# A Macaron block with its convolution by eight products for six outputs instead of six products for four

## The chip, the cores and the metric

The kernel runs on one core of a Trainium2 chip. The metric is the device time of one execution in microseconds. Time before: median 1013.6 us of three runs (1012.51 to 1014.02).

## The reference, cut to what matters

The input is one sequence of 2048 tokens of 1024 channels in fp32. The block adds half of a feed-forward layer, then a convolution with a block-wise causal attention, then half of the same feed-forward layer again:

```python
x = x + 0.5 * ffn(layernorm(x))
x = x + attention(layernorm(x))
x = x + 0.5 * ffn(layernorm(x))

def ffn(x):
    routing = softmax(x @ gate_w.T)                       # 8 experts
    return x * (routing @ in_channel_scale) @ sign(weight).T * (routing @ out_channel_scale) + bias

def attention(x):
    x = conv1d(x, conv_w, padding="SAME") + conv_b        # conv_w: (3, 1024, 768)
    q, k, v = split(x, 3, axis=-1)                        # 256 columns each
    qh, kh, vh = (project(t) for t in (q, k, v))          # 16 heads of 64
    p = softmax(causal(qh @ kh.T / 8))                    # inside blocks of 128 tokens
    return (p @ vh) @ wo + bo, projected by proj_w, plus proj_b
```

What the change touches most is the convolution of three taps from 1024 to 768 columns, between the first feed-forward layer and the attention.

## The kernel before

The program has four stages, one after the other: the first feed-forward layer (FFN1), the convolution, the attention, the second feed-forward layer (FFN2). It is written for a tile framework that follows data between the engines and orders each engine's instructions by program order and readiness; `pin(...)` keeps an instruction at its place in the program order. SyncE (SP) issues the plain transfers in its own queue order, and GpSimd (POOL) issues those that accumulate into their destination.

**FFN1** goes through 16 tiles of 128 tokens (`Ffn.run`). For each tile it normalises, transposes, routes, scales, and multiplies with the signs of the weights, `sw`, which are formed once at the start from eight loads and kept through the program. The products `pm_f` (line 286) are added to the residual row (lines 295 and 296). Behind each tile, `norm_x2` normalises the new row for the attention branch (`x2n`; its statistics in `normalize`, lines 157 to 170), and `transpose_x2` transposes it (`tr2`, line 398) into a window `xw` that holds the tile's tokens sorted by their place among four neighbours, plus one token at either end. The window is stored to DRAM (`win`), since it is needed again later.

**The convolution** is a Winograd form: from windows of inputs, six linear combinations V0 to V5 are formed on VectorE; from the three taps g0, g1, g2 of the weights, six combinations u0 to u5; the six products u_k times V_k are made on TensorE, and VectorE combines them into four neighbouring outputs. V0 and V5 (the "ends") need only g0 and g2 as weights, and their products are the groups `ce`; the others are `cv`. The 2048 tokens are processed in two halves of 1024 tokens, so a product has 256 columns. For each half, `conv_ends` makes the twelve end products (six blocks `w` of 128 output columns, two ends) while VectorE forms V1 to V4 from the reloaded windows (`load_pair`, `xl`); `conv_middle` then goes through the six blocks w with four products each, the taps of the next block (`taps`, lines 465 to 471), and the ten output operations (lines 540 to 549). All products share line 475:

```python
def product(half, acc, uk, k):
    for c in range(DC):                       # 8 chunks of 128 channels
        nc.tensor.matmul(acc..., lhsT=uk[:, c, :], rhs=V[half, k][:, :, c, :], ...)
```

V0 of the first half is formed while FFN1 runs, tile by tile (`end_transform`), and so is V5 of the first half (`store_window`).

**The attention** has four groups of 512 tokens and eight pairs of heads each, through five stages: `stage_qkv` (value products `pv`, line 716, into `vh`; query and key products `pq`, line 732), `stage_softmax`, `stage_transpose` (copies `pT`), `stage_values` (`ao`), `stage_wo`. The convolution's outputs come back from DRAM by `load_qkv`; group 0 lies in the first half. Residual rows `xr` are loaded in the second pair of each group into a ring of eight buffers (`rring`), and the result leaves as `x3`. The columns of `w` are 0 and 1 for queries, 2 and 3 for keys, 4 and 5 for values.

**FFN2** runs as FFN1 on the rows `x3`, with the same signs `sw`.

Of the kernel before, what the change touches and what calls it, by code (L numbers as in the profile page):

```python
# [24 lines left out]
def kernel(  # L25
# [52 lines left out]
    sw = fw.tile([P, DC, D], F32R, name="sw")  # L78
# [9 lines left out]
    up = pool(b1, "up", 1)  # L88
    vp0 = pool(b1, "vp0", 1)
    ends = b1.enter_context(ExitStack())  # L90
    vp5 = pool(ends, "vp5", 1, side="right")
    ring = b1.enter_context(ExitStack())
    xring = pool(ring, "xring", 8, side="right")
    xwp = pool(ring, "xwp", 3, side="right")
# [77 lines left out]
    class Ffn:  # L172
# [6 lines left out]
        def __init__(self, name, work, xnp, first, end, row, ahead, after, between, beside):  # L179
            self.name, self.work, self.xnp, self.first, self.end = name, work, xnp, first, end  # L180
            self.row, self.ahead, self.after, self.between, self.beside = row, ahead, after, between, beside
            self.xns, self.xnTs, self.lgps, self.routs, self.rTs, self.oscs, self.ys = ({} for _ in range(7))
# [95 lines left out]
        def main(self, t, *halves, between=None, at=DC - 2):  # L278
            y, osc, xrow = self.ys[t], self.oscs[t], self.row(t)
            pms = {h: bank("mm", [P, NB], f"pm_{self.name}_{t}_{h}") for h in halves}  # L280
            for c in range(DC):
                if between and c == at:
                    between()
                for h, pm in pms.items():
                    for n in range(2):
                        nc.tensor.matmul(  # L286
                            pm,
                            lhsT=y[:, n, c, :],
                            rhs=sw[:, c, ts(h, NB)],
                            start=(c == 0 and n == 0),  # L290
                            stop=(c == DC - 1 and n == 1),
                        )
# [57 lines left out]
    NK = 6  # L350
    SCALES = (1.0 / 4, -1.0 / 6, -1.0 / 6, 1.0 / 24, 1.0 / 24, 1.0)
    HALVES = 2
    TH = T // HALVES
    NQ = TH // 4
    QT = P // 4
    TPH = NT // HALVES

# [8 lines left out]
    LEFT, RIGHT = 3 * ROW - 1, QT  # L366
    AT = (LEFT, 0, ROW, 2 * ROW, LEFT + 1, 1)
    win_dram = [spill.tile([P, 2, DC, 4 * ROW], F32, name=f"win_{n}") for n in range(NT // 2)]
    x2, x2ns, xws, xls = {}, {}, {}, {}
    V = {(0, 5): vp5.tile([P, TPH, DC, QT], F32, name="v_0_5", tag="v5")}  # L370
    V |= {(half, 0): vp0.tile([P, TPH, DC, QT], F32, name=f"v_{half}_0") for half in range(HALVES)}

# [4 lines left out]
    def window(t):  # L377
        if t not in xws:
            xws[t] = xwp.tile([P, DC, 4 * ROW], F32, name=f"xw_{t}", tag="xw")
            nc.gpsimd.memset(xws[t][:, :, 2 * ROW - 1 :: 2 * ROW], 0.0)  # L380
            if t == 0:
                nc.gpsimd.memset(xws[t][:, :, LEFT : LEFT + 1], 0.0)
            if t == NT - 1:
                nc.gpsimd.memset(xws[t][:, :, RIGHT : RIGHT + 1], 0.0)
        return xws[t]
# [7 lines left out]
    def transpose_x2(t):  # L393
        xn, xw = x2ns.pop(t), window(t)
        for h in range(DC // 4):
# [3 lines left out]
            rows4 = xw[:, 4 * h : 4 * h + 4, :].rearrange("p c (k q) -> p c k q", q=ROW)  # L399
            nc.scalar.copy(rows4[:, :, :, 0:QT], tr.rearrange("p c (q k) -> p c k q", k=4))  # L400
        if t > 0:
            nc.gpsimd.tensor_copy(xws[t - 1][:, :, RIGHT : RIGHT + 1], xw[:, :, 0:1])
            store_window(t - 1)
        if t + 1 < NT:
            nc.gpsimd.tensor_copy(window(t + 1)[:, :, LEFT : LEFT + 1], xw[:, :, LEFT + QT : LEFT + ROW])
        end_transform(V[t // TPH, 0][:, t % TPH, :, :], xw, 0)
        if t + 1 == NT:
            store_window(t)

    def end_transform(v, xw, first):  # L410
        d0, d2, d4 = (xw[..., ds(at, QT)] for at in AT[first::2])
        nc.vector.scalar_tensor_tensor(v, d2, -5.0, d4, ALU.mult, ALU.add)
        nc.vector.scalar_tensor_tensor(v, d0, 4.0, v, ALU.mult, ALU.add)

    def store_window(t):
        xw = xws.pop(t)
        if t < TPH:
            end_transform(V[0, 5][:, t, :, :], xw, 1)
        nc.sync.dma_start(out=win_dram[t // 2][:, t % 2], in_=xw)

    def load_pair(n, tf):
        xls[n] = tf.tile([P, 2, DC, 4 * ROW], F32, name=f"xl_{n}", tag="xl", bufs=TPH // 2)
        nc.sync.dma_start(out=xls[n], in_=win_dram[n])

    def transform(n, k, tf):

        half, at = divmod(2 * n, TPH)
        _, d1, d2, d3, d4, _ = (xls[n][:, :, :, ds(at, QT)] for at in AT)
        v = [V[half, i][:, at : at + 2, :, :] if (half, i) in V else None for i in range(NK)]
        tmp = tf.tile([P, 2, DC, QT], F32, name=f"vt_{n}_{k}", tag="vt")  # L430
        if k == 1:
            nc.vector.scalar_tensor_tensor(v[1], d2, -4.0, d4, ALU.mult, ALU.add)
            nc.vector.scalar_tensor_tensor(tmp, d1, -4.0, d3, ALU.mult, ALU.add)
            nc.vector.tensor_tensor(v[2], v[1], tmp, ALU.subtract)
            nc.vector.tensor_tensor(v[1], v[1], tmp, ALU.add)
        else:
            nc.vector.tensor_tensor(v[3], d4, d2, ALU.subtract)
            nc.vector.tensor_tensor(tmp, d3, d1, ALU.subtract)
            nc.vector.scalar_tensor_tensor(v[4], tmp, -2.0, v[3], ALU.mult, ALU.add)
            nc.vector.scalar_tensor_tensor(v[3], tmp, 2.0, v[3], ALU.mult, ALU.add)  # L440

    def beside(t):

        if t >= NT - 3:
            for w in (2 * (t - NT + 3), 2 * (t - NT + 3) + 1):
                load_g(0, w, 0, pinned=True)
# [3 lines left out]
    def load_g(half, w, *taps, pinned=False):  # L450
        for j in taps:
            gs[half, w, j] = cwp.tile([P, DC, P], F32, name=f"g_{half}_{w}_{j}", tag="cw")
            ins = nc.sync.dma_start(out=gs[half, w, j], in_=conv_w[w, :, j])
# [3 lines left out]
    qkv_dram = [[spill.tile([P, TH], F32, name=f"qkv_{half}_{w}") for w in range(NW)] for half in range(HALVES)]  # L457

    def taps(half, w, ks):

        g = [gs[half, w, j] for j in range(3)]
        a, b = (up.tile([P, DC, P], F32, name=f"u_{half}_{w}_{k}", tag=f"u{k}") for k in ks)
        us.setdefault((half, w), {}).update(zip(ks, (a, b)))
        if ks[0] == 1:
            pin(nc.vector.tensor_tensor(a, g[0], g[2], ALU.add))
            nc.vector.tensor_tensor(b, a, g[1], ALU.subtract)
            nc.vector.tensor_tensor(a, a, g[1], ALU.add)  # L467
        else:
            nc.vector.scalar_tensor_tensor(a, g[2], 4.0, g[0], ALU.mult, ALU.add)
            nc.vector.scalar_tensor_tensor(b, g[1], -2.0, a, ALU.mult, ALU.add)  # L470
            nc.vector.scalar_tensor_tensor(a, g[1], 2.0, a, ALU.mult, ALU.add)

    def product(half, acc, uk, k):
        for c in range(DC):
            nc.tensor.matmul(  # L475
                acc.rearrange("p (t q) -> p t q", q=QT),
                lhsT=uk[:, c, :],
                rhs=V[half, k][:, :, c, :],
                start=(c == 0),
                stop=(c == DC - 1),  # L480
            )

    def leave(half, w, k, acc, mp):
        m = ms.setdefault((half, w), {})
        m[k] = mp.tile([P, NQ], F32, name=f"m_{half}_{w}_{k}", tag=f"m{k}", bufs=NW if k in (0, 5) else 1)
# [5 lines left out]
    def conv_ends(half, mp, tf, vp14):  # L491


        for k in range(1, 5):
            V[half, k] = vp14.tile([P, TPH, DC, QT], F32, name=f"v_{half}_{k}", tag=f"v{k}")
        pairs = range(half * TPH // 2, (half + 1) * TPH // 2)
        jobs = [lambda n=n: transform(n, 1, tf) for n in pairs]
        jobs += [lambda n=n: transform(n, 3, tf) for n in pairs]
        jobs += [lambda ks=ks: taps(half, 0, ks) for ks in ((1, 2), (3, 4))]
        if half > 0:  # L500
            V[half, 5] = vp5.tile([P, TPH, DC, QT], F32, name=f"v_{half}_5", tag="v5")
            ends = [V[half, 5][:, at : at + 2, :, :] for at in range(0, TPH, 2)]
            jobs = [lambda n=n, v=v: end_transform(v, xls[n], 1) for n, v in zip(pairs, ends)] + jobs
        for at in range(2 * NW):
            last, w = divmod(at, NW)
            if w % 2 == 0:
                acc = bank("mm" if at % 4 == 0 else "acc", [P, 2, NQ], f"ce_{half}_{last}_{w}")
            product(half, acc[:, w % 2, :], gs.pop((half, w, 2 * last)), 5 * last)
            leave(half, w, 5 * last, acc[:, w % 2, :], mp)
            if not last:  # L510
                load_g(half, w, 2)
            else:
                load_g(half, w // 3, w % 3)
# [421 lines left out]
```

## Time and profile before

One execution was profiled. It took 1014.76 us as a whole; the span between its first and last instruction was 1013.0 us, at a mean granted clock of 0.999.

| stage (us from the span's start) | length | TensorE busy | VectorE busy | ScalarE busy | GpSimd busy |
|---|---|---|---|---|---|
| FFN1, 0 to 200.1 | 200.1 | 185.66 | 153.43 | 113.98 | 92.64 |
| join, 200.1 to 206.9 | 6.8 | 6.06 | 3.00 | 2.75 | 1.20 |
| convolution, 206.9 to 453.9 | 247.0 | 245.76 | 174.75 | 25.75 | 0.46 |
| attention, 453.9 to 847 | 393.1 | 391.60 | 224.99 | 177.20 | 84.59 |
| FFN2, 847 to 1013 | 166.0 | 155.23 | 109.47 | 68.76 | 60.51 |

In the profile, PE is TensorE's matmuls, PEld its weight loads, DVE VectorE, ACT ScalarE, POOL GpSimd and SP SyncE. A group of instructions is given by its line, its engine, its operation, the names of what it writes and reads, the shape and the count; then follow its busy time, the mean duration of one in nanoseconds, and the idle time of its engine ahead of it with what ended it. An fp32 matmul leaves two records.

### The profile page before, as it was taken

The page shows a single profiled execution, that of the slowest core. Times are in us where ns is not written, and L with a number is a line of the kernel's source. Part 1 is how long each engine was busy: PE and PEld are TensorE (multiplying, and loading weights), DVE is VectorE, ACT ScalarE, POOL GpSimd, SP SyncE. Part 2 cuts the span into 40 slices and gives each one's busy share as a digit, 9 for nine tenths or more (in the row PEclk, how much of TensorE's full clock was granted, in tenths as well). Part 3 has the DMA queues.
Part 4 walks back from the last instruction along what each step waited for, and adds up shares of the span by engine and source line. Part 5 has one row for each costly group of instructions (what it writes and reads, how often), then busy time and mean ns, then how long its engine had stood idle before and what let it go on. Part 6 is the DMA issues. An engine that isn't in the chain of part 4 may idle for free.

```text
span 1013.0 us, 14588 instructions
## 1 busy us (share of the span) xinstructions
PE 984.3 (97%) x5420; PEld 694.8 (69%) x5420; DVE 665.6 (66%) x1243; ACT 388.4 (38%) x1074; POOL 239.4 (24%) x335
## 2 busy tenths in 40 slices
PE   5999999999999999999999999999999999899997
PEld 3778888888888888884555455545554555677776
DVE  4888887748978537756656545655565556767664
ACT  3566665410110110114445424533462552545440
POOL 3554543300000000002312211221031312543421
PEclk9999999999999999999999999999999999999999
DMA  8767554698643786217020041013003207756421
GB/s 248 221 179 210 177 169 133 226 360 294 217 158 125 226 297 213 94 46 287 1 63 1 11 156 63 1 63 104 1 1 124 73 12 208 187 147 164 106 83 63
DMA packets 39705, 139.68 MB, mean 138 GB/s; under 512 B 4617, under 2 KB 5641, under 8 KB 38610
## 3 DMA queue, kind: packets, MB, share of 16 engines
q1 hardware_dynamic: 34528, 121.65, 33.6%
q0 software_dynamic: 5088, 17.06, 9.0%
q8 instruction: 43, 0.70, 0.3%
q14 instruction: 28, 0.23, 0.1%
q10 hardware_dynamic: 18, 0.04, 0.0%
HBM read 81.84 MB, written 40.11 MB: 120 GB/s over the span
## 4 chain that ended last, share of the span: by engine, by line
PE 39%; issue 38%; DVE 10%; DMA 6%; POOL 6%; ACT 1%; POOLq 0%; DVEq 0%
PE pm_f L286 15%; PE cv L475 7%; PE ce L475 4%; POOL xr L709 3%; DMA xf<-x 3%; DMA out_dram<-xf 2%; PE pp L843 2%; PE tr_f L199 2%; DVE st_f L157 2%; POOL p L765 2%; PE acc L824 1%; PE tr L398 1%; PE lgp_f L207 1%; PE is_f L250 1%; PE pq L732 1%
## 5 line engine op out<-in xcount | busy, mean ns | idle before, releaser
L286 PE MATMUL pm_f<-sw,y_f 128*128 128x512 f32 x1024 | 265.4, 407 | 0.2 <-DVE x L296 0.2
L286 PEld LDWEIGHTS pm_f<-sw,y_f 128*128 128x128 f32 x1024 | 185.9, 190 | 40.6 <-DVE x L296 0.4
L475 PE MATMUL cv<-v,u 128*128 128x256 f32 x768 | 166.3, 379 | 0.3 <-DVE u L467 0.3
L475 PEld LDWEIGHTS cv<-v,u 128*128 128x128 f32 x768 | 145.8, 190 | 20.4 <-PE cv L475 0.7
L765 POOL TENSOR_SCALAR_AFFINE_SELECT p<-p 128x512 f32<-128x512 f32 x64 | 39.7, 644 | 507.8 <-ACT p L763 507.8
L778 ACT ACTIVATE p<-p,anm 128x128 f32<-128x128 f32 x256 | 99.0, 388 | 17.5 <-DVE anm L775 17.5
L264 POOL TENSOR_TENSOR y_f<-xnT_f,y_f 128x512 fp32r<-128x512 f32 x64 | 81.3, 1288 | 66.1 <-ACT y_f L263 65.3
L475 PE MATMUL ce<-v,g 128*128 128x256 f32 x384 | 84.3, 380 | 0.9 <-ACT m L489 0.9
L763 ACT COPY p<-sc 128x512 f32<-128x512 f32 x64 | 34.3, 588 | 127.6 <-PE sc L753 127.5
L475 PEld LDWEIGHTS ce<-v,g 128*128 128x128 f32 x384 | 72.4, 190 | 12.1 <-ACT m L489 2.3
L775 DVE TENSOR_REDUCE anm<-p 128x4 f32<-128x512 f32 x64 | 40.9, 680 | 49.5 <-POOL p L765 49.5
L824 PE MATMUL acc<-oT,wo_sb 128*128 128x512 f32 x128 | 67.7, 617 | 0.4 <-DVE oT L816 0.4
L295 DVE TENSOR_TENSOR pm_f<-pm_f,os_f 128x512 f32<-128x512 f32 x64 | 44.4, 693 | 27.9 <-PE pm_f L286 27.3
L732 PE MATMUL pq<-qkv,wq_sb 128*128 128x512 f32 x128 | 60.4, 593 | 0.0
L732 PE MATMUL pq<-qkv,wk_sb 128*128 128x512 f32 x128 | 60.1, 592 | 0.0
L843 PE MATMUL pp<-pw_sb,o2T 128*128 128x512 f32 x128 | 57.6, 600 | 0.4
L716 PE MATMUL pv<-wv_sb,qkv 128*128 128x512 f32 x128 | 56.5, 593 | 0.0
L778 ACT ACTIVATION_READ_ACCUMULATOR p<-p,anm 128x1 f32 x256 | 48.0, 187 | 0.0
L753 PEld LDWEIGHTS sc<-qk,qk 64*128 64x128 f32 x512 | 31.1, 187 | 23.7 <-issue 22.2
L786 DVE TENSOR_TENSOR p<-p,asum 128x512 f32<-128x512 f32 x64 | 45.6, 713 | 2.2
L200 ACT COPY xnT_f<-tr_f 128x512 f32<-128x512 f32 x60 | 32.5, 589 | 37.9 <-PE tr_f L199 36.1
L732 PEld LDWEIGHTS pq<-qkv,wk_sb 128*128 128x128 f32 x128 | 24.3, 190 | 30.6 <-issue 28.7
(134 smaller groups left out, 1440.9 us busy)
## 6 DMA issues: line engine op xcount, KB each, us to landing
g<-in_conv_w_dram SPq DMA_DIRECT2D x60, 512.0 KB, 4.1
win<-xw SPq DMA_DIRECT2D x16, 528.0 KB, 2.7
xl<-win SPq DMA_DIRECT2D x8, 1056.0 KB, 7.4
x<-in_x_dram SPq DMA_DIRECT2D x16, 512.0 KB, 3.8
x<-hbias POOLq DMA_DIRECT2D x16, 512.0 KB, 4.9
x<-x SPq DMA_DIRECT2D x16, 512.0 KB, 4.1
xr<-x SPq DMA_DIRECT2D x16, 512.0 KB, 6.5
x<-xr SPq DMA_DIRECT2D x16, 512.0 KB, 3.9
```

Of the source, the lines that this page charges most:

```text
L264: nc.gpsimd.tensor_tensor(yl, y, yh.bitcast(F32), ALU.subtract)
L286: nc.tensor.matmul(pm, lhsT=y[:, n, c, :], rhs=sw[:, c, ts(h, NB)], start=(c == 0 and n == 0), stop=(c == DC - 1 and n == 1),)
L295: nc.vector.tensor_tensor(pm, pm, o, ALU.mult)
L475: nc.tensor.matmul(acc.rearrange("p (t q) -> p t q", q=QT), lhsT=uk[:, c, :], rhs=V[half, k][:, :, c, :], start=(c == 0), stop=(c == DC - 1),)
L716: nc.tensor.matmul(pv, lhsT=qkvs[g][:, 2 * WC + c, ts(b, P)], rhs=wv_sb[:, c, ts(half, NB)], start=(c == 0), stop=(c == WC - 1),)
L732: nc.tensor.matmul(pq, lhsT=w_sb[:, c, ts(hp, P)], rhs=qkvs[g][:, first + c, :], start=(c == 0), stop=(c == WC - 1),)
L765: nc.gpsimd.affine_select(out=p, in_=p, pattern=[[0, BPG], [-1, P]], compare_op=ALU.is_ge, fill=NEG_INF, base=0, channel_multiplier=1,)
L775: nc.vector.tensor_reduce(nmax, p, AX.X, ALU.max, negate=True)
L778: nc.scalar.activation(p[:, b, :], p[:, b, :], AF.Exp, bias=nmax[:, b : b + 1], accum_out=asum[:, b : b + 1],)
L786: nc.vector.tensor_tensor(p, p, asum.unsqueeze(2).broadcast_to([P, BPG, P]), ALU.mult)
L824: nc.tensor.matmul(accs[g][m], lhsT=wo_sb[:, hp, ts(m, P)], rhs=oT, start=(hp == 0), stop=(hp == NHP - 1),)
L843: nc.tensor.matmul(pp, lhsT=o2T[:, m, ts(b, P)], rhs=pw_sb[:, m, ts(h, NB)], start=(m == 0), stop=(m == WC - 1),)
```

## The change

- The Winograd form goes from four outputs by six products to six outputs by eight products: NK = 8, three middle pairs of products (1,2), (3,4), (5,6), and the ends 0 and 7. A window now holds three tiles sorted by their place among six neighbours (`TRIPLES` = 6 windows; the last holds one tile), 1.6 MB each.
- There are no halves: each product takes all 2048 tokens as 342 columns. V0 and V7 are formed in FFN1 for every triple of tiles. V5 and V6 take the buffers of V0 and V7 after the end products (`last_transforms`), and the windows are loaded a second time for them.
- `WORDER` begins with the value columns: w goes 4, 5, 0, 1, 2, 3.
- The tap sums are formed partly by transfers: g0 + g2 by a load and an accumulating transfer from DRAM, 4 g2 + g0 and 4 g0 + g2 by a ScalarE multiplication and an accumulating transfer. VectorE then does two operations for each pair instead of three.
- The signs `sw` are freed after FFN1. In the third group of the attention the weights are loaded again through the ring `rring`, and their signs `sw2` are formed on ScalarE.
- In the attention both halves of `vh` of group 0 are made at its first step. The loads of `xr` and of `projb_sb` are pinned.

The core of the diff:

```diff
-    NK = 6
-    SCALES = (1.0 / 4, -1.0 / 6, -1.0 / 6, 1.0 / 24, 1.0 / 24, 1.0)
-    HALVES = 2
-    TH = T // HALVES
-    NQ = TH // 4
-    QT = P // 4
+    NK = 8
+    SCALES = (1.0, -2.0 / 9, -2.0 / 9, 1.0 / 90, 1.0 / 90, 1.0 / 180, 1.0 / 180, 1.0)
+    PAIRS = ((1, 2), (3, 4), (5, 6))
+    QT = 3 * P // 6
+    NQ = -(-T // 6)
+    TRIPLES = -(-NT // 3)
+    SIZES = [min(QT, NQ - n * QT) for n in range(TRIPLES)]
...
+    def window(n):
+        if n not in xws:
+            xws[n] = xwp.tile([P, DC, 6 * ROW], F32, name=f"xw_{n}", tag="xw")
+            if SIZES[n] < QT:
+                nc.gpsimd.memset(xws[n], 0.0)
...
+        if third == 2 or t + 1 == NT:
+            end_transform(n, 0)
+        if third == 0 and n > 0:
+            nc.gpsimd.tensor_copy(xws[n - 1][:, :, RIGHT : RIGHT + 1], xw[:, :, 0:1])
+            store_window(n - 1)
...
+    def transform(n, k, tf):
...
+        nc.vector.scalar_tensor_tensor(a, d4, f, d2, ALU.mult, ALU.add)
+        nc.vector.scalar_tensor_tensor(a, a, even, d6, ALU.mult, ALU.add)
+        nc.vector.scalar_tensor_tensor(tmp, d3, f, d1, ALU.mult, ALU.add)
+        nc.vector.scalar_tensor_tensor(tmp, d5, odd, tmp, ALU.mult, ALU.add)
+        nc.vector.scalar_tensor_tensor(b, tmp, -last, a, ALU.mult, ALU.add)
+        nc.vector.scalar_tensor_tensor(a, tmp, last, a, ALU.mult, ALU.add)
...
+    def taps(w, ks, up):
+        a, b = (up.tile([P, DC, P], F32, name=f"u_{w}_{k}", tag=f"u{k}") for k in ks)
         if ks[0] == 1:
-            pin(nc.vector.tensor_tensor(a, g[0], g[2], ALU.add))
-            nc.vector.tensor_tensor(b, a, g[1], ALU.subtract)
-            nc.vector.tensor_tensor(a, a, g[1], ALU.add)
+            pin(nc.gpsimd.dma_start(out=b, in_=conv_w[w, :, 0]))
+            nc.gpsimd.dma_start(out=b, in_=conv_w[w, :, 2], accum_op=ALU.add)
+            f = 1.0
         else:
+            four, one = (2, 0) if ks[0] == 3 else (0, 2)
+            nc.scalar.mul(b, gs[w, four], 4.0)
+            nc.gpsimd.dma_start(out=b, in_=conv_w[w, :, one], accum_op=ALU.add)
+            f = 2.0
+        nc.vector.scalar_tensor_tensor(a, gs[w, 1], f, b, ALU.mult, ALU.add)
+        nc.vector.scalar_tensor_tensor(b, gs[w, 1], -f, b, ALU.mult, ALU.add)
...
+    def last_transforms(tf, xs):
+        for k in PAIRS[-1]:
+            V[k] = ve.tile([P, DC, NQ], F32, name=f"v_{k}", tag=f"v{0 if k == 5 else NK - 1}")
+        for n, *more in ((1, 0, xwp), (2, TRIPLES - 2, xwp), (3, TRIPLES - 1, xs), (0,), (TRIPLES - 2,), (TRIPLES - 1,)):
+            transform(n, 5, tf)
+            if more:
+                load_window(*more)
...
+    for i, w in enumerate(WORDER):
+        for ks in PAIRS:
+            for k in ks:
+                product(w, k, us[w][k], mp)
+            if i == 0 and ks[0] == 1:
+                last_transforms(tf, xs)
+                wins.close()
+                taps(w, PAIRS[-1], up)
+            if ks[0] == 1 and i + 2 < NW:
+                load_g(WORDER[i + 2], 1, 2, 0)
+            if ks is PAIRS[-1]:
+                outputs(w, mp)
+            if i + 1 < NW:
+                taps(WORDER[i + 1], ks, up)
...
+    load_qkv(0, qkv0)
...
+            if g == 2:
+                raw = rring.tile([P, D], F32, name=f"raw2_{hp}", tag="x")
+                nc.sync.dma_start(out=raw, in_=weight_t[ts(hp, P), :])
+                nc.scalar.activation(sw2[:, hp, :], raw, AF.Sign)
...
-            if hp % PPV == 0:
-                half = hp // PPV
+            for half in (0, 1) if (g, hp) == (0, 0) else (hp // PPV,) if hp % PPV == 0 and (g, hp) != (0, PPV) else ():
```

## The prediction

> **What bounds the kernel now.** I read the page first: its engine totals, then the busy time of each engine by stage, then the groups of instructions in the convolution, the chain of waits around its start, and the transfers. The engine totals say that TensorE is nearly always busy:
>
> ```profile
> PE 984.3 (97%) x5420; PEld 694.8 (69%) x5420; DVE 665.6 (66%) x1243; ACT 388.4 (38%) x1074; POOL 239.4 (24%) x335
> ```
>
> The busy times by stage (columns: stretch, its length, then PE, PEld, DVE, ACT, POOL, granted clock, DMA share, GB/s) are those of the end of FFN1, of the convolution, and of the attention:
>
> ```profile
> 200.10:206.90 6.80, 6.06 (x37) 5.20 (x35) 3.00 (x7) 2.75 (x4) 1.20 (x6) 1.00 0.65 229
> 206.90:453.90 247.00, 245.76 (x1135) 214.82 (x1134) 174.75 (x260) 25.75 (x72) 0.46 (x1) 1.00 0.57 202
> 453.90:847.00 393.10, 391.60 (x2019) 206.30 (x2017) 224.99 (x399) 177.20 (x655) 84.59 (x91) 1.00 0.21 69
> ```
>
> TensorE idles 1.24 us of 247 in the convolution, 0.74 at the join before it and 1.5 of 393 in the attention. So fewer matmul columns are a gain at full price, and every new TensorE wait is a loss at full price, because no later stage has room to win it back.
>
> **TensorE work: the gain.** Three groups of the page give the price of a column. A record's "mean" includes pipelining, so I take the pitch from the weight loads: their busy time plus their idle time, over their count.
>
> ```profile
> L475 PE MATMUL cv<-v,u 128*128 128x256 f32 x768 | 166.3, 379 | 0.3 <-DVE u L467 0.3
> ...
> L475 PEld LDWEIGHTS cv<-v,u 128*128 128x128 f32 x768 | 145.8, 190 | 20.4 <-PE cv L475 0.7
> ...
> L732 PEld LDWEIGHTS pq<-qkv,wk_sb 128*128 128x128 f32 x128 | 24.3, 190 | 30.6 <-issue 28.7
> ```
>
> For 256 columns, (145.8 + 20.4) / 768 = 0.2164 us; the 257 records from 259.6 to 315.0 us agree (0.2168). For 512 columns, (24.3 + 30.6) / 128 = 0.429. Each fp32 matmul leaves two records. A line through both points gives 0.288 us for 342 columns, an estimate; no record has that width. Before: 2 halves x 6 w x 6 products x 8 chunks x 2 = 1152 records x 0.2168 = 249.8 us. After: 6 x 8 x 8 x 2 = 768 x 0.288 = 221.2 us. The change is **-28.6 us**. A product takes 16 x 0.288 = 4.61 us.
>
> **FFN1 to convolution.** Before, the products of half 0 need no late tile, and fill TensorE while the last tile is normalised. The chain of waits shows (start, duration, what):
>
> ```profile
> 203.54 0.52 POOL rs_x L164
> ...
> 204.14 0.28 POOL sh_x L169
> ...
> 204.44 1.25 ACT x2n L170
> ...
> 205.74 1.09 PE tr L398 x8
> 206.83 34.54 PE ce L475 x158
> ```
>
> After, V[0] holds all tokens, so the first product waits for this whole chain. From the last FFN1 matmul: the multiply, add and second statistics of the last half row (three DVE operations of 512 elements at 0.69), with two interleaved end-transform operations (1.4), then 0.34 for aggregation: 3.8. Next 0.52 + 0.28 + 0.1 + 1.25 = 2.15; transposes 1.09; the ACT copies with the new head and tail pieces about 1.0; three end-transform operations of 176 elements at about 0.34, or 2.7 us with the full-width ones ahead: 9.1 to 10.8. Sixteen transposes (2.1) are useful work in it and 0.74 idled before: 6.3 to 8.0. GpSimd's zeroing of the whole last window (3120 elements; an estimate of 1 to 3 us) may also stand ahead of rs_x, since its buffer is free only when an earlier window is stored. I take **+8.0** (6 to 11).
>
> **The fifth and sixth products of the first w.** V5 and V6 reuse the buffers of V0 and V7, so V6 waits for all twelve end products, and their transforms wait for windows that are loaded a second time. Vector's prices (by shape):
>
> ```profile
> L466 DVE TENSOR_TENSOR u<-u,g 128x1024 f32<-128x1024 f32 x12 | 14.7, 1225 | 10.7 <-PE cv L475 10.7
> ...
> L440 DVE SCALAR_TENSOR_TENSOR v<-vt,v 128x512 f32<-128x512 f32 x8 | 5.5, 691 | 0.2
> ```
>
> Three pairs x six windows x six operations = 108: 90 of 512 elements and 18 of 176. In the timeline 512-element operations start 0.605 us apart where independent, 0.72 where dependent, 0.663 on this mixture: 59.7. The 18 take about 0.34 (between 0.28 and 0.42 for 128 and 256): 6.1. Six tap operations at 1.22: 7.3. Sum 73.1, or 75.5 at 0.69. The second load of window 0 is issued only when Vector has finished with a buffer; only two tap operations lie between that and its use. The transfers:
>
> ```profile
> g<-in_conv_w_dram SPq DMA_DIRECT2D x60, 512.0 KB, 4.1
> win<-xw SPq DMA_DIRECT2D x16, 528.0 KB, 2.7
> xl<-win SPq DMA_DIRECT2D x8, 1056.0 KB, 7.4
> x<-hbias POOLq DMA_DIRECT2D x16, 512.0 KB, 4.9
> ```
>
> At 1560 KB the load lies between 7.4 and 10.9 (by bytes); less 2.4 of taps, Vector waits 5 to 8.5, and 1 to 3 for windows 4 and 5. V5 is then whole 79 to 87 us after the first product; TensorE has 16 products, 73.7 us. It waits 5 to 13; I take **+8.5**, nearer the low end because some transforms start before the first product.
>
> **TensorE after a long gap.** The granted clock reads 1.00 in these stages, but there is no long gap in them. The only one with work behind it is at the start (start, busy, what; idle before in brackets), set against a later row:
>
> ```profile
> 8.74 3.76 PE L199 MATMUL tr_f<-ident,xn_f 128*128 128x128 f32 x16 [4.33 <-ACT xn_f L170]
> 12.43 3.78 PE L595 MATMUL hb<-bias_row,halves 1*128 1x512 f32 x4
> ...
> 32.97 1.03 PE L199 MATMUL tr_f<-ident,xn_f 128*128 128x128 f32 x8
> ```
>
> Sixteen transposes took 3.76 against 2 x 1.03, and four records of 512 columns 3.78 against 4 x 0.429 = 1.72: a loss of 3.8. A slow stretch after the first gap is hidden, since Vector sets the time until V5; after the V5 gap it is not. Between 0 and 3.8 I take **+2.0**. The Trainium skill ("TensorE: Matmul & The Clock Gate", Part 1) speaks against a change that opens such gaps: an idle window of about 3.4 us halves the clock until about 3.4 us of work. By that rule the term would be an estimated 1.7 us and the sum 0.3 lower; the granted clock of the profile does not show the halving.
>
> **Tap sums by accumulating transfers.** Vector loses one operation per pair. The pair (1,2) of the next w starts when product 2 is done: a plain load, then an accumulating one that GpSimd issues only when the first has landed, then a tap: 4.1 + 4.9 + 1.2 = 10.2, under the cover of products 3 to 6 (18.4). Pairs (3,4) and (5,6) have one transfer each and the same cover. Cost **0**; without cover it is at most 10.2 x 5 = 51. Vector's work per w (17 output operations, at 1.34 times the 0.42 to 0.63 of before, and six taps) is about 17 us of 27.6: no bound.
>
> **Convolution to attention.** Group 0 of the attention now needs the last outputs. The v columns go first and both vh halves of group 0 (sixteen 512-column matmuls x 0.86 = 13.8 us) cover last output operations, store (3.3) and load (4.7). One evacuation on Vector stands behind the last nine output operations: 9 x 0.6, less the two pv products (3.4 us) that run before their bank is needed again, gives 2 to 3. I take **+2.7** (0 to 5).
>
> **Signs.** The second FFN's signs are formed in the attention: eight 512 KB loads queue on SP behind x3 stores and xr loads, and eight ACT operations of about 1.05 stand among the exponentials. ACT is busy 177 of 393 there, so the work is free, but a sign that waits for its load holds the pT copy behind it, and so the values on TensorE. I take **+1.0** (0 to 4).
>
> **FFN1 and FFN2.** Transforms by triples: six 512-element operations per three tiles against two to four of 256 per tile, 4.1 against 2.5 to 5.0 us per triple, and eight small ACT copies: 0 (-2 to +2). FFN2 is the same.
>
> **Sum.** -28.6 + 8.0 + 8.5 + 2.0 + 0 + 2.7 + 1.0 + 0 = -6.4. The profiled execution took 1014.76 us (span 1013.0), 1.2 above the median of 1013.6. It becomes 1008.4, and the median **1007.2 us**. With all terms at their low ends the sum is -28.6 + 6 + 5 - 2 = -19.6; with all at their high ends -28.6 + 11 + 13 + 3.8 + 5 + 4 + 2 = +10, before any transfer stalls.
>
> **Rivals.** *The waits hide.* If the reloaded window lands within the taps and the FFN1 chain overlaps, only 6 + 0 + 2 remain: -20.6, 993 us. For it: transfers ran at over 400 GB/s around 220 us. Against: Vector's 73 us equal TensorE's 73.7 without any wait. *Break-even.* Gaps of 11 and 13 with 3 to 6 behind them eat the gain: 1012 to 1015. *Accumulating transfers bind, slower than before.* Place: the pair (1,2) of each next w. It decides when both transfers plus a tap exceed 18.4, that is 8.6 us each, twice the rows above; 1056 KB loads took 7.4 at a DMA share of 0.87. At 10.0 each the wait is 2.8 per w, five times: +14, 1021 us. Against it: the share in the middle of the convolution was only 0.55.
>
> **How the numbers follow.** The forecast (sum between -14 and -2) gets 0.50; the hidden waits 0.10; break-even 0.12; binding transfers, or another wait of that size, 0.28. About 0.2% (2 us) is what a measurement can tell: faster 0.60, same 0.12, slower 0.28. The range 997 to 1021 covers the forecast, break-even, most of the binding case and the nearer part of the hidden one.
>
> **What would show it.** Records of 342 columns at 0.288 us; an idle of 6 to 11 us before the first product, released by Vector; one of 5 to 13 before the first product 5, with Vector waiting for xl; under 1 us before product 1 of later w. A pitch of 0.31, or idle before product 1 of each w, would make the prediction wrong.

## The result and the profile after

| | median | runs |
|---|---|---|
| before | 1014.05 us | 20 (1011.08 to 1016.10) |
| after | 1012.87 us | 20 (1008.74 to 1017.32) |

The ratio is 0.9991 (95% interval 0.9978 to 1.0003): no change that can be told from none. Forecast were 1007.2 us and a gain. The time lies inside the range of 997 to 1021, but the gain is not there. The new times are also more scattered (standard deviation 2.2 us against 1.2). The profiled execution of after took 1016.4 us (span 1014.3), 3.5 above its median, so its waits are on the long side.

The engine totals of the page after: TensorE has 20 us less to do than before, but the span is no shorter.

```profile
PE 964.5 (95%) x5036; PEld 626.3 (62%) x5036; DVE 656.6 (65%) x1231; ACT 407.6 (40%) x1112; POOL 258.8 (26%) x328
```

What TensorE waited for from the end of FFN1 to the start of the attention (engine, line, for what; us in total, times, longest):

```profile
PE cv L504 <- DVE v L459: 12.6, 1, 12.6
PE tr L401 <- ACT x2n L168: 6.5, 1, 6.5
PE cv L504 <- DVE v L434: 3.1, 1, 3.1
PE pv L752 <- DVE vh L762: 1.6, 1, 1.6
```

The same stretch of before had only short waits: 0.74 us at the join, two of at most 0.5 and one of 0.3 in the convolution. The second and third lines are the join with FFN1; the first is the wait before product 5 of the first w, from 288.76 to 301.40 us. The busy times by stretch show what followed both (the granted clock is the third number from the end):

```profile
200.00:212.00 12.00, 2.41 (x13) 1.77 (x11) 7.86 (x18) 3.74 (x9) 3.99 (x6) 0.67 0.77 280
212.00:220.00 8.00, 8.00 (x18) 4.95 (x19) 8.00 (x18) 0.26 (x1) 0.00 (x0) 0.64 0.91 365
260.00:300.00 40.00, 28.75 (x100) 18.55 (x98) 24.15 (x39) 5.17 (x9) 3.17 (x4) 0.91 0.97 321
300.00:340.00 40.00, 38.60 (x126) 25.19 (x127) 22.47 (x36) 5.18 (x9) 3.13 (x4) 0.92 0.57 156
```

Before, all four read 1.00. By the trace's clock records it is 0.50 from 204.1 to 217.7 us and from 292.8 to 306.5, 13.65 us each time. The DMA engines are full (0.97) just where V5 is formed.

What V5 waited for stands in VectorE's timeline. V5's last operation, on 176 elements, starts at 300.91; the operation ahead of it is a tap of the *second* w, which waits 7.21 us for a transfer:

```profile
292.24 0.33 DVE L458 SCALAR_TENSOR_TENSOR v<-vt,v 128x176 f32<-128x176 f32 x1
299.77 1.23 DVE L495 SCALAR_TENSOR_TENSOR u<-g,u 128x1024 f32<-128x1024 f32 x1 [7.21 <-DMA u<-in_conv_w_dram]
300.91 0.34 DVE L459 SCALAR_TENSOR_TENSOR v<-vt,v 128x176 f32<-128x176 f32 x1
```

GpSimd's timeline has the pair of transfers behind it: the load goes out when product 2 frees its buffer, the accumulating one 10 us later, when the first has landed, and that one lands another 9.6 us later.

```profile
279.84 0.55 POOL L487 DMA_DIRECT2D u<-in_conv_w_dram  x1 [17.33 <-PE cv L504]
290.10 0.86 POOL L488 DMA_DIRECT2D u<-in_conv_w_dram  x1 [9.70 <-DMA u<-in_conv_w_dram]
```

The 24 transfers of this kind ("software transfers" below: those that GpSimd issues) landed in a median of 6.3 us, so this pair, at 10.0 and 9.6 us, was late.

### The profile page after: what moved, and what is told of

It is laid out like the page before. It is cut to its first block, busy times and chain, and to the rows that moved or that the text cites. A ratio compares the mean times of both kernels' runs of the same rounds, so it can differ in the third digit from the quotient of the medians.

```text
span 1014.3 us, 13802 instructions
## 1 busy us (share of the span) xinstructions
PE 964.5 (95%) x5036; PEld 626.3 (62%) x5036; DVE 656.6 (65%) x1231; ACT 407.6 (40%) x1112; POOL 258.8 (26%) x328
## 4 chain that ended last, share of the span: by engine, by line
issue 36%; PE 30%; POOL 5%; DMA 4%; DVE 3%; ACT 1%; POOLq 0%; DVEq 0%
PE cv L504 12%; PE pm_f L284 9%; POOL xr L745 3%; PE pp L879 2%; DMA u<-in_conv_w_dram 2%; POOL p L801 2%; PE acc L860 1%; DMA xf<-x 1%; DMA out_dram<-xf 1%; PE tr_f L197 1%; PE pq L768 1%; DVE st_f L155 1%; PE ao L843 1%; PE is_f L248 1%; PE lgp_f L205 1%
## 5 line engine op out<-in xcount | busy, mean ns | idle before, releaser
L504 PE MATMUL cv<-v,u 128*128 128x342 f32 x576 | 168.8, 455 | 12.6 <-DVE v L459 12.6
L504 PEld LDWEIGHTS cv<-v,u 128*128 128x128 f32 x576 | 110.3, 192 | 70.9 <-issue 15.0
L510 ACT ACTIVATE m<-cv 128x342 f32<-128x342 f32 x42 | 19.2, 457 | 177.3 <-PE cv L504 167.1
L504 PE MATMUL cv<-v,g 128*128 128x342 f32 x192 | 58.4, 467 | 3.1 <-DVE v L434 3.1
L495 DVE SCALAR_TENSOR_TENSOR u<-g,u 128x1024 f32<-128x1024 f32 x18 | 22.0, 1224 | 53.8 <-DMA u<-in_conv_w_dram 24.3
L504 PEld LDWEIGHTS cv<-v,g 128*128 128x128 f32 x192 | 37.8, 197 | 23.6 <-DVE v L434 3.5
```

What stands on the lines that cost most here:

```text
L504: nc.tensor.matmul(acc, lhsT=uk[:, c, :], rhs=V[k][:, c, :], start=(c == 0), stop=(c == DC - 1))
```

## The experiments

The first theory was A: the wait before product 5 is mainly an order in VectorE's queue, and the half clock adds to it. Rivals were Vector's own work, the window loads, and crowded transfers. Ratios are against the kernel before on the same chip, to be set beside 0.9991 of the change. Its repeat e3, further down, gave 1.0002, so a difference of 1 us says nothing.

**Order (e1).** One tap operation is issued behind V5's last operation:

```diff
-            if i + 1 < NW:
+            if i == 0 and ks[0] == 1:
+                with tc.issue_after(whole.ins):   # V5's last operation
+                    taps(WORDER[i + 1], ks, up)
+            elif i + 1 < NW:
                 taps(WORDER[i + 1], ks, up)
```

> Edit: on VectorE alone, the tap operation of the second w (u 5_1, waiting for two software transfers) is issued behind the last operation of V5 instead of one place ahead of it. Nothing else moves. Theory A (the wait of 12.6 us before product 5 is a queue order: V5 is whole at about 292.6 us but for one operation of 0.34 us behind that tap): TensorE waits about 4 us there instead of 12.6, less of the stretch after it is at half clock, and the time falls by 8 to 11 us against the changed kernel, to 1002 to 1005 us. Theory B (the wait is the reload of the windows and Vector's own work): the last operation of V5 was only a bystander, 0 to -1 us. Theory C (the second w's taps then become the wait before product 1 of the second w, since their transfers land at 299.7): the wait moves there, at most -4 us.

Measured: 1013.0 us, 0.9969 (0.9947 to 0.9991). That is 2 to 3 us, not 8 to 11. In its profile the tap no longer stands ahead, yet TensorE still waits 10.4 us: VectorE waits 2.49 and 2.34 us for software transfers of the first w, and 4.04, 1.91 and 1.76 us for windows. The one operation was the last of several late things, and in this execution the pair had landed by the time the tap was issued, without a wait. Theory A in this form falls.

**Pair (1,2) on VectorE (e2).**

```diff
         if ks[0] == 1:
-            pin(nc.gpsimd.dma_start(out=b, in_=conv_w[w, :, 0]))
-            nc.gpsimd.dma_start(out=b, in_=conv_w[w, :, 2], accum_op=ALU.add)
+            nc.vector.tensor_tensor(b, gs[w, 0], gs[w, 2], ALU.add)
```

> Edit: the sum g0 + g2 of pair (1,2) of every w is made by one more VectorE operation of 1024 elements from the taps that are in SBUF anyway, instead of a load and an accumulating transfer (12 software transfers of 512 KB less). Theory A (the serial pair of transfers, 9.7 + 9.6 us in the profile, holds the tap operation ahead of V5's last): the wait before product 5 falls from 12.6 to about 5 to 6, -7 to -10 us, 1003 to 1006 us. Theory B (VectorE's own 73 us bind): six more operations of 1.2 us cost, +1 to +2 us. Theory C (the wait is set by window loads): fewer bytes in flight, -1 to -3 us.

Measured: 1009.0 us, 0.9934 (0.9911 to 0.9956). Product 5 waits 1.3 us for a tap and 2.8 for V5, 4.1 together, a little less than theory A had. The attention starts 10 us earlier in the profiles (441.5 against 451.4), of which the whole time keeps about 6 (forecast were 7 to 10).

**Weight loads (e3).**

```diff
-        if i == 1:
+        if i == 3:
             aw = pool(b2, "aw", 1, side="right")
```

> Edit: the three loads of 1 MB of the attention's weights are issued two w later, so that they do not run beside the transfers at 280 to 300 us. Theory A1 (the accumulating transfer of 9.6 us is slowed by crowding; DMA share 1.02 there): it lands in about 6 us, the wait before product 5 falls by 3 to 4 us, and so does the time, 1009 us. Theory A2 (a software accumulate takes that long by itself): 0 us. The loads must then land before 451 us, or the first value products wait.

The edit left the order of every engine as it was, so this run is a repeat of the changed kernel: 1015.45 us, 1.0002 (0.9986 to 1.0017), its wait before product 5 being 7.9 us. There the load of the software pair landed in 4.1 us, not 10.0, and the tap ahead of V5's last operation waits for nothing; VectorE waits 6.2 us for the first w's software transfers and 6.6 for windows. So the same order gives waits of 7.9 to 12.6 us. What differs is which transfer goes out first, the software load or the second loads of windows (`xl`); the change first, then e3:

```profile
278.59 3.23 SPq L442 DMA_DIRECT2D xl<-win  x2
...
280.72 3.23 SPq L442 DMA_DIRECT2D xl<-win  x2
279.89 0.56 POOL L487 DMA_DIRECT2D u<-in_conv_w_dram  x1 [17.19 <-PE cv L504]
```

In the change the load follows at 279.84. In the three profiles with the windows ahead (the change, e4, f4) the load lands in 9.4 to 10.0 us; in the three with the load ahead (e1, e3, g3) it lands in 4.1. No run sets this order on purpose, so it is a match in six profiles, not a proof.

**Busy TensorE (e4).**

```diff
+    def warm(n, name):
+        d = bank("tr", [P, NQ], f"warm_{name}")
+        for _ in range(n):
+            pin(nc.tensor.matmul(d, lhsT=ident, rhs=hbias[:, 0:NQ], start=True, stop=True))
...
     transpose_x2(NT - 2)
+    warm(10, "a")
     transpose_x2(NT - 1)
+    warm(4, "b")
...
+                if i == 0 and k == 5:
+                    warm(18, "c")
```

> Edit: TensorE runs matmuls of 342 columns that nobody reads, ten and four in the two waits before the convolution (6.5 and 3.1 us) and 18 in the wait before product 5 (12.6 us), 0.57 us each, so that it is busy there. Theory A (after each wait TensorE runs at half clock, 5.8 and 5.3 us long, and this is paid): granted clock 1.00 from 200 to 310 us, about 2.9 + 0.9 us back before the ends of product 2, on which the second w's transfers wait, and 2.7 after the gap: -5.5 to -6.5 us, 1006.5 to 1007.5. Theory B (only the second gap's slow stretch is on the path): -2.7 us. Theory C (the granted clock of the records does not set the time): 0 or slightly slower.

Measured: 1012.66 us, 0.9972 (0.9953 to 0.9992), 3 us below e3 and 2 below the change's own ratio, with intervals that overlap. The granted clock reads 1.00 throughout:

```profile
200.00:212.00 12.00, 10.49 (x42) 6.67 (x41) 9.17 (x21) 2.49 (x6) 3.31 (x5) 1.00 0.83 301
300.00:340.00 40.00, 40.00 (x140) 26.29 (x140) 24.70 (x38) 7.08 (x12) 3.99 (x5) 1.00 0.58 147
```

The end products take 55.55 us instead of 58.40, and the attention starts at 443.8; from the end of FFN1 to there the profile is 6.4 us shorter, as theory A has it. So the half clock is real and paid in this stretch, but the whole time gains half of what was expected or less, which theory B's 2.7 us would fit as well.

**All taps on VectorE (f1).** As e2, and for the other pairs:

```diff
-            nc.scalar.mul(b, gs[w, four], 4.0)
-            nc.gpsimd.dma_start(out=b, in_=conv_w[w, :, one], accum_op=ALU.add)
+            nc.vector.scalar_tensor_tensor(b, gs[w, four], 4.0, gs[w, one], ALU.mult, ALU.add)
```

> Edit: all three tap sums of every w on VectorE (three operations of 1024 elements per pair, as before the change); no software transfer and no ScalarE multiplication for taps. 24 transfers of 512 KB fewer. Theory A (what holds V5 are transfers that take 8 to 10 us each because the stretch from 260 to 300 us is crowded, DMA share 1.0; the accumulating ones cause much of it and VectorE stands in order behind them): the wait before product 5 falls from 12.6 to 2 to 4 us, V5 as early as with pair (1,2) alone on VectorE or 1 to 2 us earlier; 1006 to 1009 us on a chip where the kernel before takes 1014.5. Theory B (VectorE, at 18 us of 27.6 per w, gets 3.7 us more and becomes late): waits before product 1 of later w, slower than the variant with pair (1,2) alone by 2 us or more.

Measured: 1002.89 us, 0.9885 (0.9870 to 0.9899), 11 us below the change, more than expected. The wait before product 5 is 0.9 us, and no later product 1 waits. VectorE's waits from 205 to 300 us are now these; after the change it waited 13.1 us for u transfers and 4.3 for windows there (a wait of 4.1 at the join, the same in both, is left out):

```profile
DVE u L491 <- PE cv L502: 3.4, 1, 3.4
DVE u L487 <- DMA g<-in_conv_w_dram: 0.7, 1, 0.7
...
DVE v L454 <- DMA xl<-win: 0.3, 1, 0.3
```

**The same transfers, unread (h1).** The kernel of f1, and beside each pair's taps:

```diff
+        nc.gpsimd.tensor_copy(junk[:, 0, 0:1], after[:, 0:1])   # after: the product that freed u
...
+        nc.gpsimd.dma_start(out=junk, in_=conv_w[w, :, 2, 0:nj], accum_op=ALU.add)
```

> Edit on the kernel with all tap sums on VectorE (1002.9 us beside 1014.6): GpSimd issues the 24 software transfers again, at about their old times, into buffers that nobody reads (12 of 512 KB, 12 of 384 KB); VectorE's order is the same as without them. Theory A (the transfers did their harm as traffic: they delayed the window loads that V5 waits for): VectorE waits for windows again before V5, TensorE 3 to 8 us before product 5, and the time is 4 to 8 us longer, 1007 to 1011. Theory B (they did it as something VectorE's queue waits for): nothing waits for them now, under 1 us longer, 1003 to 1004.

Measured: 1004.87 us, 0.9906 (0.9878 to 0.9934), 2 us above f1, the intervals overlapping: between the two theories, nearer to B. VectorE waits 3.1 us for windows, TensorE 2.3 before product 5 (0.9 in f1); the DMA share from 260 to 300 us is 0.94 against 0.68. The traffic makes the windows later, by less than theory A said. Half of the transfers are a quarter smaller than the old ones, so the traffic is not quite the same. Of the 11 us, some 2 came back with it; the rest goes with VectorE standing in order behind software transfers, and with the slow stretch that followed: neither f1 nor h1 shows a clock of 0.50 behind the wait before product 5.

**Second try at the weight loads (g3).**

```diff
-            wv_sb, wq_sb, wk_sb = (load_rows(...) ...)
+            with tc.issue_after(left.ins):            # the second w's store
+                wv_sb, wq_sb, wk_sb = (load_rows(...) ...)
```

> Edit on the changed kernel: the three loads of 1 MB of the attention's weights are queued on SP behind the store of the second w's outputs (in the earlier try they stayed where they were, and that run is a repeat of the changed kernel). Accumulating transfers stay. Theory A (the transfers at 280 to 300 us are slow because the stretch is crowded): the second window loads and the accumulating pair land 3 to 4 us earlier, the wait before product 5 falls from 12.6 to about 9, total -3 to -4 us. Theory B (software transfers are slow by themselves, 8 us or more): 0 to -1 us.

Measured: 1013.83 us, 0.9987 (0.9970 to 1.0004): the change's own ratio. The share from 260 to 300 us falls from 0.97 to 0.83, but the u transfers' median is 6.7 us, no shorter. Product 5 waits 7.8 us, which is no sign of theory A, since the repeat e3 has 7.9 without the edit. The time fits theory B, but not its reason: the pair's load landed in 4.1 us here, its accumulating transfer in 10.1.

**V5 due later (f2).** Pair (1,2) on VectorE as in e2, and the order of products of the first two w:

```diff
+    turn = [(i, ks) for i in range(NW) for ks in PAIRS]
+    turn[2], turn[3] = turn[3], turn[2]
+    for i, ks in turn:
...
+        if i == 0 and ks[0] == 1:
+            taps(WORDER[1], ks, up)
+            last_transforms(tf, xs)
```

The second w's taps thus go to VectorE ahead of V5's operations, and the results m1 and m2 get a second buffer each.

> Edit: pair (1,2) on VectorE as before, and TensorE does products 1 and 2 of the second w before products 5 and 6 of the first (two more buffers for m1 and m2). V5 is then needed 9.2 us later. Theory A (apart from its queue order, V5 is simply due too early: 4.1 us of wait are left with pair (1,2) on VectorE): no wait before product 5, -4 to -5 us against that variant (1009.0), 1004 to 1005. Theory B (the taps of the second w now come too late, since VectorE works on V5 and V6): a wait of 2 to 4 us before product 1 of the second w takes its place, 0 to -2 us.

Measured: 1003.23 us, 0.9881 (0.9865 to 0.9896). No product waits for V5; two wait for taps, 2.7 us together, of which 1.0 falls on the second w's product 1, so part of theory B holds as well. It is 5 us below e2.

**With a busy TensorE (f3).** The edits of f2 and e4's first two groups of matmuls.

> Edit: as the interleaved variant, and TensorE runs 14 matmuls that nobody reads in the two waits ahead of the convolution (6.5 and 3.1 us). Theory A (the half clock of 5.8 us after those waits is hidden as long as V5 sets the time, and is paid once V5 does not): -3 to -4 us against the interleaved variant, 1000 to 1002 us. Theory B (V5 still sets the time): 0 us.

Measured: 1000.55 us, 0.9861 (0.9846 to 0.9876), 2.7 us below f2 by medians with intervals that overlap: near theory A.

**Signs without loads (f4).**

```diff
-                raw = rring.tile([P, D], F32, name=f"raw2_{hp}", tag="x")
-                nc.sync.dma_start(out=raw, in_=weight_t[ts(hp, P), :])
-                nc.scalar.activation(sw2[:, hp, :], raw, AF.Sign)
+                nc.scalar.activation(sw2[:, hp, :], hbias, AF.Sign)
```

> Edit on the changed kernel: the second FFN's signs are formed from a row block that is in SBUF instead of from reloaded weights, so the eight loads of 512 KB in the attention are left out, and with them the right signs; the eight ScalarE operations stay. Theory A (the attention is 1.6 to 3.7 us longer than before because the signs wait for loads, the pT copy stands behind them, and the value products wait for it: 1.4 to 2.3 us in three of five profiles): no wait of the value products for pT, attention 1.5 to 2.5 us shorter, total -1.5 to -2.5 us. Theory B (the ScalarE operations themselves delay the pT copies): 0 us.

This kernel leaves out the weights' real signs, so only its times mean something. Measured: 1021.72 us, 1.0068 (1.0054 to 1.0083), against both theories. With nothing to wait for, all eight signs were issued at the start of the attention, and the vh copy that TensorE needs stood behind them:

```profile
449.75 7.67 ACT L736 ACTIVATE sw<-hbias 128x1024 fp32r<-128x1024 f32 x8
457.32 0.57 ACT L758 COPY vh<-pv 128x512 f32<-128x512 f32 x1
```

That wait is 5.2 us. The value products' waits for pT are gone, as theory A has it, but the edit moved more than it took away and does not settle the price.

**All together (g1: the edits of f1, f2 and e4's first two groups), then the signs two steps behind their loads (g2).**

> Edit: all tap sums on VectorE, products 1 and 2 of the second w before 5 and 6 of the first, and 14 unread matmuls in the two waits ahead of the convolution: three edits tried singly or in pairs before, now together. Theory A (each takes away another of the three losses: transfers that crowd and hold VectorE's queue, V5 due too early, half clock): 0.9 us of wait before product 5 and 0.8 + 1.7 before the second w's taps go, and 3 us of half clock; 996 to 999 us where the kernel before takes 1014.5. Theory B (with all taps on VectorE, its work is again what V5 or a tap waits for): no better than 1000.5.

Measured: 999.97 us, 0.9845 (0.9823 to 0.9867), between theory A's 996 to 999 and theory B's 1000.5. TensorE waits nowhere between the first product and the attention, but the median is hardly below f3: the attention and FFN2 take 567.4 us there, against 564.6 in f3 and 559.2 before.

```diff
+            at = g * NHP + hp - 2 * NHP - 2
+            if 0 <= at < NHP:
+                pin(nc.scalar.activation(sw2[:, at, :], raws.pop(at), AF.Sign))
```

> Edit on the one before: in the third group of the attention each sign is formed two steps after its row block is loaded, instead of in the same step; nothing is left out. Theory A (the value products wait 1.4 to 2.9 us for pT copies that stand on ScalarE behind signs whose loads have not landed): those waits fall under 0.5 us and the time by 1.5 to 2.5 us. Theory B (the ring of eight buffers, not the order, delays the loads): the waits stay, 0 us.

Measured: 997.49 us, 0.9822 (0.9799 to 0.9845). The wait of the value products for pT (2.4 us in g1) is gone. This version, which keeps the eight products for six outputs, beats both kernels: 1.8% below before.

## Why the prediction was right or wrong

- **Fewer columns: right.** A record of 342 columns starts 0.288 us after the last (112.75 us for 391 records from 338.82); forecast 0.288. The gain of 28 us is there.
- **Join with FFN1: right.** 9.59 us of idle against 0.74, +8.9; forecast 8.0. GpSimd's zeroing of the last window took 2.71 us, inside the bound.
- **Tap sums by accumulating transfers: the step that failed.** It was put at 0, since 10.2 us of transfers and tap lay under 18.4 us of products. Taking them out gave 11 us (f1). The working asked only when TensorE would need the taps. It did not ask what VectorE, which takes its instructions in order, does meanwhile: in the first w it is itself the bound, and each tap that waits for a transfer holds V5. In all six profiles that kept the transfers (the change, e1, e3, e4, f4, g3) it waits 4.8 to 6.2 us for the first w's own taps, and in three of them 7.0 to 7.2 more for the second w's. The landing times were too low there too: 10.0 and 9.6 us against the 4.1 and 4.9 that were taken.
- **The wait before product 5: inside its bounds, for the wrong reason.** 12.6 us against 5 to 13, but the windows cost VectorE 4.3 us there, not 6 to 11.5, and the u transfers 13.1. In the repeat e3 it is 7.9 us, with 6.6 for windows and 6.2 for u transfers: near the 8.5 that was taken, by luck, since the u transfers stood at nothing.
- **After a long gap: too small.** Forecast 2.0, with the first gap's slow stretch hidden. Products from 211.92 to 451.41 took 226.85 us without the wait, 5.7 more than 768 x 0.288, and eight transposes 1.97 instead of 1.09: 6.5 us. The first stretch was not hidden, since the second w's transfers start only when the first w's product 2 is done. Whether the whole 6.5 shows in the time is less sure: e4 gave 2 to 3. The prediction noted that the profile before shows no halving at its start; but that profile's clock records begin at 30.4 us, and those of e1, which begin at 12.4, have 0.50 from 15.8 to 26.1 us.
- **Convolution to attention:** 1.6 us (forecast 2.7). **Signs:** no wait for pT in the profile after, 1.3 to 2.9 us in the ten variants that kept the loads and their order (forecast 1.0, 0 to 4); g2 is 2.5 us below g1, with overlapping intervals.
- **The rival that ended slower** named the right pair of transfers and a landing over 8.6 us, but had TensorE wait for it in every w; in the later w the pair lands in 3.7 to 7.3 us each and nothing waits for it. The rival of break-even gave the right time nearly by its own terms (gaps of 11 and 13 with 3 to 6 behind them): a gap of 9.6, one of 12.6, and 8 behind them.

Added up in the profiles: -28.6 of products, +8.9, +12.6, +6.5 and +1.6 are +1.0. The attention and FFN2 are longer by 3.7 us, 2.1 more than the wait at their start; FFN1 is 0.7 shorter, and about 1 us of idle in the convolution before is gone. That makes +1.4; the executions differ by +1.6. Against the forecast sum of -6.4 the profile is 8.0 us worse: 4.1 are the wait before product 5 and 4.5 the slow stretches, and what else missed nearly cancels. The 2.1 us have no wait row of their own. With the same matmuls of the two traces set side by side, each counted from its start of the attention, the new one is 1.9 us late early in the attention, 2.5 in the last of its four groups and 3.4 at the start of FFN2. A slow stretch from 869.7 to 873.1 us, behind a gap of 2.34 us that before has too without one, adds 1.4, which the rest of FFN2 takes back. The length varies between profiles (559 us before, 563 to 568 after and in the variants with the signs' loads), and why stays open.

The Trainium skill ("TensorE: Matmul & The Clock Gate", Part 1) has the half clock begin after at least one idle window of about 3.4 us and end after at least one busy one, and it calls these windows free-running: they do not start with the kernel's own work. The traces agree with that: the stretches at 0.50 behind gaps last 3.41, 6.83, 10.24 or 13.65 us, whole multiples of 3.41. So the half clock begins and ends at no fixed distance from the work. Here it begins 3.7 and 4.1 us after the last matmul and lasts for 5.8 and 5.1 us of products; over all gaps of 5 us and more from the join on, in all profiles, that is 2.0 to 5.4 and 2.9 to 6.1 us. Where it begins after 2.0 us, the trace does not bear out a whole idle window.

## What to carry to other kernels

A transfer that replaces an operation is not free because its result is needed late: look at which in-order engine waits for it, and whether that engine has something due sooner queued behind. In the stretch where an engine builds what the next stage needs, keep from its queue whatever waits for a transfer, or give the consumer other work first. When TensorE's columns shrink by a tenth, every join that had been hidden needs its own cover, and a gap can cost a slow stretch on top: here every gap of 5 us or more, from the end of FFN1 on, did, and some gaps of 2.3 to 2.8 us.

## What the runs showed of the hardware

- In and after each of the two gaps the granted clock stood at 0.50 for 13.65 us, and 5 to 6 us of products ran at that rate; in the other profiles such stretches last 3.41, 6.83, 10.24 or 13.65 us. A gap of 2.34 us in FFN2 lowered the clock in the profile after and not in before. 32 unread matmuls in the gaps kept it at 1.00 (e4).
- In the profile after, software transfers of 512 KB from DRAM landed in 3.7 to 10.4 us (plain) and 5.2 to 12.9 us (accumulating). A DMA share of 0.83 instead of 0.97 did not shorten their median (6.7 us in g3, 6.3 in the profile after). A load issued about 1 us behind a window load landed in 9.4 to 10.0 us (three profiles), one issued about 1 us ahead of it in 4.1 (three).
- The same order of instructions gave waits before product 5 of 12.6 and 7.9 us in two profiles, with the same pair of transfers landing in 10.0 and 9.6 us in the one and in 4.1 and 10.5 in the other (e3).
